# Local attention's values by two products and transfers, the common expert's first quarter in the tail of the chunked streams, and ScalarE's table loads placed by the planner

## The chip, the cores and the metric

The kernel runs on one core of a Trainium2 chip, in one launch. The metric is the device time of a launch in microseconds (us), the median of several runs. A profiled execution, from which all spans, waits and busy times are read, is a launch of its own with a time of its own. The engines are TensorE (PE, with its weight loads PEld), VectorE (DVE), ScalarE (ACT), GpSimd (POOL) and SyncE (SP), which here only issues transfers.

## The reference

The input is `x` of 8 sequences by 256 tokens by 128 channels (float32). Four layers follow each other, each an attention part and a feed-forward part, and each part ends in `x = layernorm(x + part(x))`. Some parts read the same 2048 tokens under another grouping.

```
L0 attn   gated linear recurrence (rglru), 4 x 512 tokens
L0 ffn    2 layers: local attention (8 heads of 64, window 64), then a gated MLP (gelu)
L1 attn   selective scan (mamba): exp(delta A), 16 states per channel
L1 ffn    32 experts, top 1, capacity 80
L2 attn   chunked streams: attention + ffn in chunks of 32 (la, lf), then across chunks (sa, pf)
L2 ffn    8 experts, top 2, capacity 320, and a common expert for every token
L3 attn   16 heads of 8, rotary and decay by head type, causal
L3 ffn    one matrix, quantized to -a, 0, +a
```

Two pieces matter here. Local attention, where a window of 64 queries sees its own 64 keys and the 64 before them:

```
q, k, v = split(shift_token(x) @ wqkv)
sim  = q_window . [k_window_before, k_window]      (masked: i < j or i > j + 64)
out  = softmax(sim) @ [v_window_before, v_window]
```

And the common expert of the L2 feed-forward, which reads all 2048 tokens and adds its result to that of the routed experts:

```
shared = silu(x @ sg) * (x @ su) @ sd              sg, su: 128 x 1024, sd: 1024 x 128
```

## The kernel before

**Stages.** The program is written as generators, one for each stage, which yield between steps: `rglru`, then local attention and the scan together (`local_mamba`, to about 800 us of the profile), `moe1`, `chunked` (to about 1270 us), `moe2`, and `typed`, which ends the kernel. `x` lies as channels by tokens (128 x 2048) in SBUF.

**Order.** Instructions are not issued in the order of the text. The class `_Order` collects all operations with their dependencies and makes a plan by list scheduling, with durations from a table (`LENGTHS`), a bias for each kind of operation and stage (`BIAS`), and a time that an engine stays with one kind of tile or one table (`STAY`). `impose` then chains each engine's operations in the planned order. So a change of one number in these tables may move instructions in every stage, and a queue, that of SP's transfers too, issues strictly in its planned order: an instruction that waits holds up all behind it. PSUM banks are handed out by stage and letter (`self.psum("Q", "vps")`); `chunked` has three of K, two of A, one of B and two of M, and `moe2` two of A, two of B, three of M and one of S.

**Local values.** `local_attention` runs for 2 layers by 8 sequences, 16 blocks of 256 tokens. Queries come in two tiles of 128. The first tile sees keys 0 to 127; in the second one the first 64 queries see keys 64 to 191 and the last 64 see keys 128 to 255. Keys on partitions are needed for the second product (`o`), so the values of keys 0 to 127, 64 to 191 and 128 to 255 are made by three products `vps`, each copied by ACT into a third of `v` (L1123 to 1128). The loads of `bc` that the scan of mamba multiplies with (L1269, 128 loads of 256 KB) stand in SP's queue in the same stage.

**The tail of `chunked` and `moe2`.** `chunked` passes 8 sequences through la, lf, sa and pf, several in flight. Each ends with `normed`, a transposition `zt`, the copy `x_chunked`, and the logits of the router (`lg`, then the positions by `cum`). After the last sequence come its scatters into `places` (POOL), two reads of `places` each (`got<-places`, some issued by ACT), the transposes `bt`, and the 8 experts (`pg<-bt`, `pu`, `py`). The common expert is made in four quarters of 512 tokens by `shared(i)`, a generator inside `moe2`: 8 chunks of 128 hidden channels, each of two products 128x512 (`pg`, `pu`), a Silu (ACT, L2052), a multiplication (DVE, L2057) and four products that add into one bank, `acc`. Quarter 0 covers the routing of the last sequence; quarters 1 to 3 come after the experts. During quarter 1 the gathers of the experts' results (`got<-ybuf,get`, POOL, L1658, 32 in this stage) are paced one a chunk by `fetch`; during quarters 2 and 3 the first sequence of `typed` is begun.

**Tables of ACT.** Exp and Ln share a table set; Silu, Gelu and Sigmoid each need another. A change of set puts an `ACT_TABLE_LOAD` into ACT's queue. Before Silu, Gelu or Sigmoid it is put in by itself; for Exp and Ln the text asks for the load by hand, with `exp_ln` (L900), right after the last activation of the other set, and `keep` holds it there.

Of the kernel before, what the change touches and what calls it, by code (L numbers as in the profile page):

```python
# [23 lines left out]
P = 128  # L24
B = 8
S = 256
# [55 lines left out]
def _tables():  # L82
# [65 lines left out]
    madd("band", np.concatenate([mask((i < k0) | (i > k0 + 64)), mask((k0 < w) | (k0 > w + 64))], 1))  # L148
# [163 lines left out]
class _Order:  # L312
# [14 lines left out]
    STAY = dict(PE=80, ACT=740)  # L327
    BIAS = {
        "ACT  1": 100, "ACT  5": 585, "ACT bt 3": 5, "ACT bt 5": -775, "ACT d 2": -425, "ACT da 2": -45, "ACT e 2": -5, "ACT e 4": 965, "ACT e 6": -20,
        "ACT got 3": 575, "ACT h 2": -200, "ACT ix 4": 15, "ACT k 2": 265, "ACT lavp 2": 210, "ACT lnrs 1": -10, "ACT lnrs 2": -160, "ACT lnsq 1": -135,  # L330
        "ACT lnsq 2": 15, "ACT ot 2": 10, "ACT ptsb 2": -595, "ACT ptsb 6": -515, "ACT q 2": 20, "ACT qsq 2": 10, "ACT r 2": -5, "ACT rg 1": 10,
        "ACT rg 2": -915, "ACT rn 2": 15, "ACT rs 4": 340, "ACT rs 6": -690, "ACT s 6": 200, "ACT sakq 2": -10, "ACT sg 3": -550, "ACT sh 5": -2525,
        "ACT spe 1": -220, "ACT spt 1": -50, "ACT st 6": 100, "ACT sz 2": 280, "ACT v 2": 885, "ACT vs 4": 320, "ACT xchunked 2": 15, "ACT xs 2": -610,
        "DVE biasfull 3": -335, "DVE biaspart 3": -20, "DVE bt 5": -5, "DVE c 1": 590, "DVE centre 0": 320, "DVE d 2": 10, "DVE decaypart 4": -600,
        "DVE e 4": 570, "DVE four 4": 100, "DVE fs 4": -70, "DVE gate 4": 340, "DVE get 2": 200, "DVE got 4": 530, "DVE identb 0": -50, "DVE k 6": 500,
        "DVE lg 2": 2240, "DVE lo 4": -265, "DVE mv 4": -660, "DVE mv 5": 100, "DVE mv 6": -485, "DVE nm 2": -3975, "DVE nm 6": 4960, "DVE nth 4": -45,
        "DVE oh 2": -725, "DVE oh 5": -10, "DVE ptsb 2": -3895, "DVE ptsb 6": 895, "DVE put 4": -395, "DVE put 5": 55, "DVE q 5": -825, "DVE q 6": -475,
        "DVE rc 2": -1225, "DVE rc 6": 10, "DVE route 2": -55, "DVE s 5": 10, "DVE sares 2": 70, "DVE sel 2": -1590, "DVE sg 3": -140, "DVE sm 4": 2720,
        "DVE spl 1": -215, "DVE ss 2": 370, "DVE st 4": 85, "DVE st 6": 1645, "DVE sum 4": 170, "DVE t 2": 440, "DVE u 2": 250, "DVE vs 4": 50,
        "DVE we 4": 1425, "DVE xc 2": 460, "DVE xla 4": -15, "DVE xlocal 2": -5, "DVE xmoe 5": -200, "DVE xmoe 6": -580, "DVE xpf 4": -370,  # L340
        "DVE xrglru 2": 120, "DVE xsa 4": 80, "DVE z 4": -1990, "PE a 2": -100, "PE acc 5": 155, "PE b 2": -35, "PE bt 3": 75, "PE bt 5": 50,
        "PE cum 2": -995, "PE cum 4": -25, "PE cum 5": -615, "PE fold 2": 2915, "PE g 2": -4155, "PE gate 2": 785, "PE kps 4": 135, "PE less 2": 295,
        "PE lg 2": 1680, "PE lg 4": 50, "PE ln 2": -10, "PE o 2": 10, "PE o 6": -10, "PE pg 5": 150, "PE ps 4": -15, "PE pt 4": -130, "PE pu 3": 220,
        "PE py 3": -200, "PE py 5": 170, "PE qk 2": 25, "PE qkt 2": -720, "PE raw 2": -8675, "PE rows 2": 400, "PE sc 2": -50, "PE sc 4": 65, "PE sc 6": 5,
        "PE v 5": 290, "PE vps 2": 4075, "PE vps 4": 25, "PE wo 2": 75, "PE wo 6": -85, "PE wout 2": -115, "PE xin 2": 1180, "PE xps 2": -2540, "PE y 2": 20,
        "PE z 2": -450, "PE zt 5": 560, "PE zt 6": 25, "POOL d 2": 130, "POOL e 6": -30, "POOL got 4": -200, "POOL h 2": 370, "POOL k 5": 400,
        "POOL k 6": 850, "POOL km 6": 1240, "POOL mean 0": 1510, "POOL places 5": -200, "POOL q 6": 20, "POOL rest 4": -65, "POOL rg 1": -800,
        "POOL rg 2": -200, "POOL rot 2": -400, "POOL s 6": -750, "POOL t 2": 550, "POOL zero 0": -655, "POOL zeros 1": 385, "SP bc 2": -970, "SP cst 3": 5,
        "SP got 3": 355, "SP got 5": 350, "SP rottable 0": 80, "SP rows 4": 210, "SP rowschunked 4": -105, "SP vec 0": -830, "SP w 0": 15, "SP w 3": 115,
        "SP wattn 2": 585, "SP wffn 2": 705, "SP wlocal 0": 1175, "SP wmoe 4": 520, "SP xs 2": -105, "SP ybuf 5": -200,  # L350
    }
    LENGTHS = {
        "ACT  LoadActFuncSet  ": (1178, 1283), "ACT d Ln 128x512 128x512": (535, 640), "ACT da Exp 128x255 128x255": (398, 503),
        "ACT e Abs 128x256 128x256": (460, 565), "ACT e Exp 128x128 128x128": (420, 525), "ACT e Exp 128x256 128x256": (461, 566),
        "ACT e Exp 128x512 128x512": (527, 632), "ACT four Exp 128x2 128x2": (100, 205), "ACT got DMACopy 128x512 128x512": (454, 3611),
        "ACT h TensorCopy 64x255 64x255": (295, 400), "ACT lnrs Exp 128x256 128x256": (315, 420), "ACT ot TensorCopy 128x512 128x512": (486, 591),
        "ACT qsq Square 128x512 128x512": (494, 599), "ACT r Relu 128x256 128x256": (460, 565), "ACT rg Exp 128x1020 128x1020": (1039, 1144),
        "ACT rg Exp 128x1024 128x1024": (998, 1103), "ACT rg Ln 128x1024 128x1024": (950, 1055), "ACT rn Exp 128x16 128x16": (110, 215),
        "ACT rn Ln 128x16 128x16": (112, 217), "ACT rs Exp 128x2 128x2": (96, 201), "ACT rs Ln 128x2 128x2": (98, 203),
        "ACT sh Silu 128x512 128x512": (492, 597), "ACT v TensorCopy 128x512 128x512": (485, 590), "ACT xc Identity 128x256 128x256": (460, 565),  # L360
        "ACT xc Silu 128x512 128x512": (526, 631), "ACT xchunked TensorCopy 128x256 128x256": (263, 368), "ACT xmoe Identity 128x256 128x256": (404, 509),
        "ACT xs TensorCopy 33x256 33x256": (257, 362), "ACT xsq Square 128x128 128x128": (297, 402), "DVE biaspart TensorCopy 96x256 96x256": (197, 282),
        "DVE decay TensorScalarPtr 128x512 128x512": (508, 593), "DVE decaypart TensorCopy 128x512 128x512": (331, 416),
        "DVE four TensorScalarPtr 128x4 128x4": (76, 160), "DVE ge TensorScalarPtr 128x256 128x256": (380, 465),
        "DVE ge TensorScalarPtr 85x256 85x256": (372, 457), "DVE got TensorScalarPtr 128x128 128x128": (258, 343),
        "DVE h TensorTensor 128x256 128x256": (312, 397), "DVE hs TensorScalarPtr 128x1024 128x1024": (2189, 2274),
        "DVE hs TensorTensor 128x1024 128x1024": (1116, 1201), "DVE mv BNStatsAggregate 128x2 128x6": (82, 167),
        "DVE nm TensorTensor 128x8 128x8": (66, 151), "DVE ptsb TensorCopy 128x512 128x512": (589, 674), "DVE rc Reciprocal 128x16 128x16": (160, 245),
        "DVE rc Reciprocal 128x4 128x4": (84, 169), "DVE rc Reciprocal 128x8 128x8": (106, 191), "DVE rg TensorScalarPtr 128x256 128x256": (577, 662),
        "DVE rg TensorTensor 128x1024 128x1024": (1109, 1194), "DVE rottable TensorScalarPtr 128x256 128x256": (261, 346),  # L370
        "DVE s TensorScalarPtr 128x128 128x128": (247, 332), "DVE s TensorTensor 128x256 128x256": (323, 408),
        "DVE sm TensorReduce 128x16 128x512": (593, 678), "DVE ss TensorReduce 128x8 128x512": (594, 679), "DVE st BNStats 128x6 128x128": (197, 282),
        "DVE sum TensorReduce 128x32 128x448": (810, 895), "DVE t TensorScalarPtr 128x256 128x256": (384, 469),
        "DVE t TensorTensor 128x512 128x512": (593, 678), "DVE vec TensorTensor 128x1 128x1": (59, 144), "DVE vec TensorTensor 85x1 85x1": (59, 144),
        "DVE vs TensorCopy 128x512 128x512": (594, 679), "DVE wlocal TensorScalarPtr 128x682 128x682": (481, 566),
        "DVE x TensorScalarPtr 128x256 128x256": (368, 453), "DVE xc TensorScalarPtr 128x254 128x254": (383, 468),
        "DVE xc TensorScalarPtr 128x255 128x255": (384, 469), "DVE xla TensorScalarPtr 128x256 128x256": (442, 527),
# [65 lines left out]
    def group(self, i):  # L443
# [5 lines left out]
        if e == "ACT":  # L449
            return 1 if op == "LoadActFuncSet" else self.SETS.get(str(x.func).split(".")[-1]) if op == "Activation" else None  # L450
        return None

    def change(self, i):
        x, e, op = self.ops[i]
        if e == "ACT":
            return 0.0 if op == "LoadActFuncSet" else self.TABLE
# [315 lines left out]
class _Kernel:  # L772
# [125 lines left out]
    def exp_ln(self, last=None):  # L898

        i = self.nc.scalar.preload_act_table_set("natural_log_exp_and_others")  # L900
        if last is not None:
            self.issue_after([i], last)
# [1508 lines left out]
```

## Time and profile before

| | |
|---|---|
| median of 3 runs | 1628.3 us (1627.46 to 1633.44) |
| profiled execution | 1644.68 us, span 1642.9 us |
| granted clock of PE, mean | 0.942 |
| busy PE / DVE / ACT / POOL | 1417.4 / 1102.3 / 968.6 / 587.5 us |
| table loads in the five largest groups of them | 30, 16, 7, 3 and 2 |
| moved by DMA | 77.97 MB, mean 47 GB/s |

A row of the groups reads: line, engine, operation, out<-in, shapes, count, then busy time in us and the mean in ns of one, then the idle time of the engine ahead of them and what ended most of it. "L870" is the helper that issues every matmul, so its rows are told apart by their tiles. A float32 product of 128x512 shows as two MATMUL rows. In a timeline a row has its start, its length, the engine and the operation, and in brackets the idle time before it and its releaser.

### The profile page before, as it was taken

The numbers are of one execution on the slowest core, as the hardware profiler recorded it, in microseconds if no ns is written. First come the engines' busy times: TensorE is split into PE (matmuls) and PEld (weight loads), VectorE is DVE, ScalarE is ACT, GpSimd is POOL, SyncE is SP. The second block draws the span as 40 slices with busy tenths as digits, with TensorE's granted clock in tenths as the row PEclk, the third lists the DMA queues.
The fourth block names the chain that finished last, engine by engine and source line by source line (L and its number), as shares of the span: only waits on it lengthen the run. The fifth ranks groups of instructions, "written<-read, shape, count | busy, mean of one in ns | idle before, by whom it ended". The sixth has DMA issues, their size and how long they took to land. (4 is left out here: it accounts for less than half of the span.)

```text
span 1642.9 us, 28581 instructions
## 1 busy us (share of the span) xinstructions
PE 1417.4 (86%) x10826; PEld 909.4 (55%) x10826; DVE 1102.3 (67%) x2182; ACT 968.6 (59%) x2656; POOL 587.5 (36%) x535
## 2 busy tenths in 40 slices
PE   2688998989898887777579999999998899899997
PEld 1354554545554544334366766777675576556664
DVE  5745568898989898698545557554546333279886
ACT  3777888787978869446125545455453222167775
POOL 1334544535462523101431222212212102467774
PEclk7789999989999999779789999999998899999998
DMA  5000012121212223155430000000000130000000
GB/s 199 1 1 1 1 40 65 40 60 45 65 40 65 53 52 91 52 179 189 151 119 1 8 12 11 10 5 8 32 18 24 46 121 26 26 9 8 5 8 11
DMA packets 45113, 77.97 MB, mean 47 GB/s; under 512 B 5580, under 2 KB 21988, under 8 KB 43824
## 3 DMA queue, kind: packets, MB, share of 16 engines
q1 hardware_dynamic: 39648, 70.02, 14.0%
q0 software_dynamic: 3216, 5.07, 1.1%
q8 instruction: 85, 1.39, 0.4%
q10 hardware_dynamic: 2112, 1.05, 0.2%
q14 instruction: 52, 0.43, 0.1%
HBM read 66.87 MB, written 10.76 MB: 47 GB/s over the span
## 5 line engine op out<-in xcount | busy, mean ns | idle before, releaser
L870 PE MATMUL y<-hs,ident 128*128 128x512 f32 x256 | 139.7, 659 | 35.9 <-DVE hs L1307 35.6
L1158 POOL TENSOR_TENSOR e<-e,rc 128x1024 f32<-128x1024 f32 x32 | 78.0, 2437 | 202.7 <-DVE rc L1157 194.3
L1306 DVE TENSOR_TENSOR_SCAN hs<-da,hs 128x1024 f32<-128x1024 f32 x64 | 149.1, 2331 | 0.2
L2259 ACT ACTIVATE e<-sc,nm 128x128 f32<-128x128 f32 (+1 forms) x256 | 105.2, 427 | 46.6 <-DVE nm L2254 40.3
L1153 ACT ACTIVATE e<-sc,nm,rn 128x128 f32<-128x128 f32 x256 | 114.3, 466 | 13.8 <-DVE nm L1148 13.5
L981 PE MATMUL pt<-ident,e 128*128 128x128 f32 x768 | 114.2, 278 | 9.4 <-POOL e L1158 4.9
L1302 ACT ACTIVATE da<-d,na 128x255 f32<-128x255 f32 x256 | 109.3, 504 | 17.5 <-DVE hs L1306 13.7
L1836 POOL TENSOR_TENSOR e<-e,rc 128x512 f32<-128x512 f32 x32 | 34.0, 1064 | 219.8 <-DVE rc L1835 154.2
L981 PEld LDWEIGHTS pt<-ident,e 128*128 128x128 f32 x768 | 88.5, 141 | 42.5 <-issue 16.1
L2262 POOL TENSOR_TENSOR e<-e,rc 128x1024 f32<-128x1024 f32 x48 | 90.8, 1896 | 39.1 <-DVE rc L2261 32.1
L1105 POOL TENSOR_TENSOR t<-t,t 128x512 f32<-128x512 f32 x64 | 83.9, 1316 | 58.0 <-DVE t L1092 51.6
L1811 ACT COPY kp<-kps 128x512 f32<-128x512 f32 x128 | 74.7, 583 | 49.0 <-PE kps L870 46.4
L1658 POOL DMA_INDIRECT got<-ybuf,get x48 | 45.7, 952 | 159.2 <-DMA ybuf<-ys 97.1
L870 PEld LDWEIGHTS y<-hs,ident 128*128 128x128 f32 x256 | 48.5, 205 | 82.5 <-DVE hs L1307 54.2
L1304 DVE TENSOR_TENSOR hs<-u,bc 128x1024 f32<-128x1024 f32 x64 | 84.3, 1328 | 2.9 <-POOL u L1291 2.9
L1307 DVE TENSOR_TENSOR hs<-hs,bc 128x1024 f32<-128x1024 f32 x64 | 80.6, 1260 | 0.0
L1847 ACT COPY vs<-vps 128x512 f32<-128x512 f32 x64 | 37.4, 585 | 67.1 <-PE vps L870 53.6
L983 DVE COPY ptsb<-pt 128x512 f32<-128x512 f32 x104 | 68.8, 675 | 11.6 <-PE pt L981 9.3
L870 PE MATMUL qk<-w_local,h 128*128 128x512 f32 x128 | 69.3, 631 | 7.5 <-DVE t L1092 7.1
L870 PE MATMUL vps<-sa_vp,x_lf 128*32 128x512 f32 x512 | 68.4, 594 | 0.0
L1847 DVE COPY vs<-vps 128x512 f32<-128x512 f32 x64 | 43.3, 682 | 37.2 <-PE vps L870 25.1
L2057 DVE TENSOR_TENSOR sh<-sh,pu 128x512 f32<-128x512 f32 x32 | 22.0, 688 | 67.1 <-PE pu L870 54.0
(380 smaller groups left out, 3782.4 us busy)
## 6 DMA issues: line engine op xcount, KB each, us to landing
bc<-xs SPq DMA_DIRECT2D x128, 256.0 KB
w_moe<-in_e_dram SPq DMA_DIRECT2D x16, 768.0 KB
w_attn<-in_w_dram SPq DMA_DIRECT2D x4, 1024.0 KB
w_local<-in_w_dram SPq DMA_DIRECT2D x2, 1557.0 KB
places<-zeros SPq DMA_DIRECT2D x2, 1280.0 KB
got<-places SPq DMA_DIRECT2D x6, 256.0 KB
ybuf<-ys SPq DMA_DIRECT2D x8, 160.0 KB
x_in<-in_x_dram SPq DMA_DIRECT2D x1, 1024.0 KB
```

The source lines that it names most:

```text
L870: return self.nc.tensor.matmul(out, lhsT, rhs, start=start, stop=stop)
L981: self.last = self.nc.tensor.transpose(pt[:, j * P : (j + 1) * P], src[:, j * P : (j + 1) * P], self.ident)
L1105: nc.gpsimd.tensor_add(t1, t1, t2)
L1153: nc.scalar.activation(e[:, j, g, :], scs[:, j, g, :], AF.Exp, bias=nm[:, j, g : g + 1], scale=rq[:, j, g : g + 1], accum_out=sm[:, j, g : ...
L1158: nc.gpsimd.tensor_tensor(e, e, rc.unsqueeze(3).to_broadcast([P, 2, 4, P]), ALU.mult)
L1302: nc.scalar.activation(da[:, n, c, 1:S], d[:, c, 1:S], AF.Exp, scale=na[:, i : i + 1])
L1304: nc.vector.tensor_tensor(hs, u.unsqueeze(1).to_broadcast(shp), bn, ALU.mult)
L1306: nc.vector.tensor_tensor_scan(line(hs), line(da), line(hs), 0.0, ALU.mult, ALU.add)
L1307: nc.vector.tensor_tensor(hs, hs, cn, ALU.mult)
L1847: i = copy(v[:, c, :, :].rearrange("p a b -> p (a b)"), ps)
L2259: nc.scalar.activation(e[:, i, :], sc[:, i, :], AF.Exp, bias=nm[:, i : i + 1], accum_out=sm[:, i : i + 1])
L2262: nc.gpsimd.tensor_tensor(e, e, rc.unsqueeze(2).to_broadcast([P, n, keys]), ALU.mult)
```

## The change

**Local values.** Only keys 0 to 127 and 128 to 255 are multiplied and copied (two products). The middle tile is put together by two transfers from SBUF to SBUF on SP's queue, each of 64 partitions by 512: keys 64 to 127 go to partitions 64 to 127, where they already lie, and keys 128 to 191 to partitions 0 to 63, where they lie. The middle tile so has its halves swapped; the `k` columns of the second query tile's first half are read with halves swapped, and its half of the mask `band` is rolled by 64.

**Common expert.** `shared` becomes a method. Quarter 0 is made as `early` inside `one_sequence` for the last sequence of `chunked`, in `chunked`'s banks K and M, in steps between that sequence's `ffn`, `normed` and `x_chunked`; its sum lies in a part added to the tile of the weights. In `moe2`, quarter 1 stands where quarter 0 stood, quarters 2 and 3 after the experts; the gathers are paced two a chunk in quarter 2 and one in quarter 3, and the first sequence of `typed` begins in quarter 3.

**Tables.** `exp_ln`, `keep` and the loads by hand go. The planner counts a load for each change of set, and `impose` puts one in where ACT's planned order turns to Exp or Ln.

**Planner.** `BIAS` and `LENGTHS` are replaced (some 200 numbers); `STAY` goes from PE 80 and ACT 740 to PE 170 and ACT 530 ns.

```diff
     w = i % 64
-    madd("band", np.concatenate([mask((i < k0) | (i > k0 + 64)), mask((k0 < w) | (k0 > w + 64))], 1))
+    late = mask((k0 < w) | (k0 > w + 64))
+    late[:64] = np.roll(late[:64], 64, 1)
+    madd("band", np.concatenate([mask((i < k0) | (i > k0 + 64)), late], 1))
...
-    STAY = dict(PE=80, ACT=740)
+    STAY = dict(PE=170, ACT=530)
...
     def impose(self):
         order, _ = self.plan()
+        ring, last = [], None
+        for i in order["ACT"]:
+            g = self.groups[i]
+            if g is not None:
+                if g == 1 != last:
+                    load = self.tc.nc.scalar.preload_act_table_set("natural_log_exp_and_others")
+                    self.ops.append((load.ins, "ACT", "LoadActFuncSet"))
+                    ring.append(len(self.ops) - 1)
+                last = g
+            ring.append(i)
+        order["ACT"] = ring
...
-            self.exp_ln(nc.scalar.activation(xc, xc, AF.Silu))
+            nc.scalar.activation(xc, xc, AF.Silu)
...
         v = pools.tile([P, 3, 512], F32, tag="v", name="v")
-        for a in range(3):
+        for t in range(2):
             ps = self.psum("Q", "vps")
-            self.mm(ps, h[:, 64 * a : 64 * a + P], w[:, l, 1024:1536])
-            nc.scalar.copy(v[:, a, :], ps)
+            self.mm(ps, h[:, t * P : (t + 1) * P], w[:, l, 1024:1536])
+            half = slice(64 - 64 * t, P - 64 * t)
+            nc.scalar.copy(v[:, 2 * t, :], ps)
+            nc.sync.dma_start(v[half, 1, :], v[half, 2 * t, :])
...
-                        self.mm(scs[q0 - t * P : q0 - t * P + n, j, g, :], q[r, g, q0 : q0 + n], k[r, g, k0 : k0 + P], False, g == 3)
+                        keys = k[r, g, k0 : k0 + P]
+                        if k0 == 64:
+                            keys = keys.rearrange("p (a b) -> p a b", a=2)[:, ::-1, :]
+                        self.mm(scs[q0 - t * P : q0 - t * P + n, j, g, :], q[r, g, q0 : q0 + n], keys, False, g == 3)
...
+                early = iter(())
                 if b == B - 1:
                     self.weights_shared()
+                    self.norm = None
+                    early = self.shared(0, y, self.s0, work, ("K", "M"), tag="e", bufs=4)
...
+                next(early, None)
                 z = yield from self.ffn(x3, w[:, 1, :], "pf", add, work, small)
+                next(early, None)
+                next(early, None)
                 zt = self.by_channel(z)
...
+                next(early, None)
                 yield 0.3, 0.6
...
                 z = self.normed(out[:, 0:2, :], work, small, "z")
+                next(early, None)
+                next(early, None)
                 yield 0.3, 2.5
...
                 nc.scalar.copy(y[:, cs], self.by_channel(z))
+                for _ in early:
+                    pass
                 yield 0.3, 0.8
...
+    def shared(self, i, x, s, work, banks=("A", "S"), tag="sh", bufs=None):
+        gu, down = self.wsh
+        acc = self.psum(banks[1], "acc")
+        nc.sync.dma_start(s, self.zrows[512 * i : 512 * (i + 1), :].rearrange("(t p) d -> p t d", p=P))
+        for c in range(8):
+            pg, pu = self.psum(banks[0], "pg"), self.psum(banks[0], "pu")
+            self.mm(pg, gu[:, 0, c * P : (c + 1) * P], x[:, cs])
+            self.mm(pu, gu[:, 1, c * P : (c + 1) * P], x[:, cs])
+            h = work.tile([P, 512], F32, tag=tag, name="sh", bufs=bufs)
+            self.silu = nc.scalar.activation(h, pg, AF.Silu)
...
+            self.paced = nc.vector.tensor_mul(h, h, pu)
+            for t in range(4):
+                ts = slice(t * P, (t + 1) * P)
+                self.mm(acc[:, ts], h[:, ts], down[:, c * P : (c + 1) * P], c == 0 and t == 0, c == 7 and t == 3)
+            yield
...
-            common = shared(0)
+            common = shared(1)
...
-            for _ in shared(1):
-                next(fetch)
             self.x = y
             first = chain(results(0, self.ty), self.typed_before(0))
             for i in (2, 3):
                 for _ in shared(i):
-                    next(first, None)
+                    next(fetch, None)
+                    if i == 3:
+                        next(first, None)
                     next(fetch, None)
```

## The prediction

> **What bounds the kernel now.** I read the page's busy shares first, then the busy time in windows cut by stage, then the groups of the edited lines, then the timelines of TensorE (PE) and ScalarE (ACT) in the tail of `chunked`.
>
> ```profile
> PE 1417.4 (86%) x10826; PEld 909.4 (55%) x10826; DVE 1102.3 (67%) x2182; ACT 968.6 (59%) x2656; POOL 587.5 (36%) x535
> 100.00:240.00 140.00, 124.69 (x888) 76.75 (x887) 78.59 (x141) 112.10 (x316) 62.42 (x72) 0.99 0.01 4
> 300.00:600.00 300.00, 263.27 (x1531) 156.10 (x1532) 270.35 (x337) 247.75 (x649) 140.90 (x121) 0.98 0.21 57
> 1249.90:1273.50 23.60, 16.73 (x87) 11.49 (x87) 18.91 (x115) 8.63 (x34) 8.48 (x10) 0.82 0.15 41
> 1273.50:1300.80 27.30, 22.02 (x97) 13.88 (x96) 8.16 (x24) 6.85 (x11) 7.93 (x9) 0.84 0.27 70
> 1360.00:1442.00 82.00, 73.10 (x328) 47.19 (x326) 25.79 (x54) 18.59 (x29) 34.09 (x35) 0.94 0.10 28
> ```
>
> The first line is the page's, the others are windows (stretch, its length, then busy time of PE, PEld, DVE, ACT, POOL, the granted clock, DMA). PE leads the whole, but not every stage. From 100 to 240 us, local attention before the scan, PE is busy 89% of the time, ACT 80%, VectorE (DVE) 56%: a product taken away there shortens the stage. From 300 to 600 us the scan runs beside it: DVE 90%, PE 88%, ACT 83%. A product saved there mostly becomes idle time of PE. The tail of `chunked` (1249.9 to 1273.5, one sequence left) has PE at 71% and ACT at 37%: here lies room for other work.
>
> ```profile
> L870 PE MATMUL vps<-w_local,h 128*128 128x512 f32 x96 | 52.4, 642 | 6.7 <-ACT v L1128 5.8 <-DVE t L1092 0.9
> L1128 ACT COPY v<-vps 128x512 f32<-128x512 f32 x48 | 28.0, 594 | 12.9 <-PE vps L870 12.7
> L900 ACT ACT_TABLE_LOAD x30 | 38.5, 1283 | 0.5
> L2052 ACT ACTIVATE sh<-pg 128x512 f32<-128x512 f32 x32 | 19.1, 597 | 76.4 <-PE pg L870 56.6 <-remote 11.5 <-issue 6.3
> ```
>
> Groups (count, busy us and mean ns, idle before and its releaser). A 128x512 product is two matmul rows: 96 rows for 48 products. The copies of `v` cost 594 ns, a table load 1283 ns, a Silu 597 ns. Silu waits for PE, hence PE bounds the common expert.
>
> ```profile
> 1275.13 0.20 ACT L1606 ACTIVATE four<-four 128x2 f32<-128x2 f32 x1 [3.56 <-DVE four L1605]
> 1275.35 1.28 ACT L2052 ACT_TABLE_LOAD   x1
> 1276.64 0.60 ACT L2052 ACTIVATE sh<-pg 128x512 f32<-128x512 f32 x1
> 1282.44 1.02 ACTq L1643 DMA_DIRECT2D got<-places  x2
> 1283.50 0.60 ACT L2052 ACTIVATE sh<-pg 128x512 f32<-128x512 f32 x1 [6.26 <-issue]
> 1277.29 2.08 PE L870 MATMUL pg<-x_chunked,w_shared 128*128 128x512 f32 x2 [3.58 <-ACT sh L2052]
> ```
>
> ACT's and PE's timelines. The first Silu of the common expert waits for the last exp of the routing and a load; the second waits 6.26 us, since ACT's queue holds the two reads of `places` until the scatters have landed. PE stands 3.58 us here and its clock was granted at 0.50 from 1265 to 1282. So 50.9 us (1249.9 to 1300.8) pass from the tail's last `zt` to the experts, with 38.75 us of PE work at a mean clock of 0.83.
>
> ```profile
> 1411.11 1.02 PE L870 MATMUL pg<-x_chunked,w_shared 128*128 128x512 f32 x2
> 1411.97 1.02 PE L870 MATMUL pu<-x_chunked,w_shared 128*128 128x512 f32 x2
> 1412.17 0.60 ACT L2052 ACTIVATE sh<-pg 128x512 f32<-128x512 f32 x1 [2.01 <-PE pg L870]
> 1414.78 0.60 ACT L2052 ACTIVATE sh<-pg 128x512 f32<-128x512 f32 x1 [2.01 <-PE pg L870]
> ```
>
> In steady state a product steps by 0.86 us (1411.97 - 1411.11) and a chunk by 2.61 us (1414.78 - 1412.17). A quarter has 8 chunks: 20.9 us, all PE.
>
> **Local values.** 16 blocks (2 layers, 8 sequences) lose one product and one copy each: 16 x 0.86 = 13.8 us of PE, 16 x 0.594 = 9.5 us of ACT. The built order also has five loads fewer before `chunked` (65 to 60): 6.4 us of ACT. Eight blocks have their products before 245 us, where PE decides: 8 x 0.86 x 0.89 (PE's share) = 6.1 us gained. For the other eight DVE is as busy as PE; between nothing and 6.9 us I take a quarter, 1.7. Sum -7.8. The best end is all of the product time and the loads, -13.8 - 6.4 = -20.2: one row speaks for the loads, PE's 4.29 us of idle at 61.1 us, waiting for a copy of `v` while ACT does six loads in 14 us.
>
> Added are 32 transfers of 128 KB on SP's queue. Issue: the 256 KB loads of `bc` took a median of 0.42 us each there, so 13.6 us on a queue that does little else. Landing: the trace has no such transfer; the nearest is the reading of `places` (256 KB), issued at 1282.4 with its transposes at 1288.6, at most 6.2 us. The cover: in before's 16 blocks 8.7 to 40 us lie between the last copy of `v` and the first `o` product of the second query tile, which is what needs the moved rows. So the landing costs nothing; with the cover gone it is 6.2 us a block at most. The swapped halves and the rolled mask change no size of a product. The wait that is added: each transfer stands in SP's order behind its ACT copy, and behind it stand loads of `bc` that DVE's scan needs. Those loads are double-buffered (they wait for DVE, 175 us in all), so I price this at zero; the bad end is a rival below.
>
> **First quarter in the tail.** Let X be the time from 1249.9 to the last routing product `cum`, 23.6 us now. In the built order all 8 pairs of products and the 32 `acc` products of quarter 0 stand before that `cum`, and ACT goes back and forth 7 times between Silu and exp/ln: 14 loads in place of none. ACT's work: 8.63 + 14 x 1.283 + 8 x 0.597 = 31.4 us. PE's: 16.73, less the one chunk already there (four rows from 1269.9, about 3.6), plus 20.9: 34 us at the worst clock seen, some 31 at full clock. So X is at least 31.4; with every load and Silu put onto the chain it is 23.6 + 18.0 + 4.8 = 46.4. Between them neither engine excludes either end; I take the middle, 38.9. From `cum` to the experts 27.3 us stay: 8 scatters in a row on POOL (1.27 us each), the reads, the transposes; quarter 1 now covers them as quarter 0 did (22.0 us of PE work in them now, 20.9 of it a quarter's). Then behind the experts two quarters are left of three: -20.9. Sum 38.9 + 27.3 - 50.9 - 20.9 = -5.6; ends -13.1 (X = 31.4) and +1.9 (X = 46.4). The products wait in banks of `chunked` (two of three K, one of two M), so the sequence's own `ffn` and transposes are served by what is left: part of why I do not take 31.4. The weights' loads were issued at 1184 and 1193 us, 57 us ahead: no cost.
>
> A load's price is the row's 1283 ns: the Silu starts 0.01 us after it, and the load 0.02 us after the exp. The Trainium skill speaks against this interleaving ("ScalarE: Activation LUTs", sections "What ACT_TABLE_LOAD costs" and "Table sets: the hidden batching unit"): it puts a switch at about 2.7 us with its drain, and has calls batched by set. By that the 14 loads would be 37 us, the serial X 65, and this part a loss of some 21 us at that end. The trace shows no drain, so the row goes into the sum.
>
> **Gathers.** 32 gathers step by 1.25 us (0.95 and 0.30 of issue): 40 us from 1381.6, beside 62.7 us of quarters. Now they run beside 41.8 us, two a chunk, and the first sequence's `q`, `k`, `km` stand among them on POOL. They come in order of sequence, so only some start late: 0 to 3 us, I take 1. Loads behind the experts lie beside an ACT that is busy 18.6 of 82 us: nothing.
>
> **New order.** Biases and stays are retuned, so every stage is reordered; built tile-shape switches of PE rise by some 20. No row prices an order; the longest single wait of PE for the scan (`y` after `hs`) is 5.2 us, and one such wait more or less is what I allow, +-5, centre 0.
>
> Sum: -7.8 - 5.6 + 1 = -12.4. The profiled execution took 1644.7 us (span 1642.9 and 1.8 around it), 16.4 above the median; one stall in it (ACT 11.5 us, "remote", near 1391 to 1403) I neither credit nor count. It would go to 1632.3; as a difference from the median: 1628.3 - 12.4 = **1616**.
>
> **Rivals.** (1) Everything gains: -20.2 - 13.1 + 1 = -32, so 1596. For it: ACT and PE are both lightened at once in the first stage, and PE's half clock in the tail goes when it is fed. Against: DVE at 90% from 300 to 600 us.
> (2) One half gives nothing: the local products hide behind the scan and the new order (1623), or X comes out at 44.5, where the tail neither gains nor loses (1621). For it: the serial X of 46.4.
> (3) SP's queue, slower:
>
> ```profile
> SPq L1269 <- DMA xs<-xs: 9.5, 8, 2.2
> L1269 SPq DMA_DIRECT2D bc<-xs x128: 319/423/1637, 236.9 to 779.0; - x128
> ```
>
> (waits of SP's queue: us in all, times, longest; and the `bc` loads, ns min/median/max, first and last start.) The eight blocks beside the scan put 16 transfers among these 128 loads. If each holds the next `bc` for the longest landing wait seen, 2.2 us, DVE loses 35 us: -12.4 + 1.7 + 35 = +24, 1653. It turns the change into a loss from 0.7 us per transfer, and by over 0.5% from 1.2. Against: the loads are issued ahead.
> (4) The change does not save table loads, as it says it plans them: the built count rises from 69 to 76. That is in X.
>
> **Numbers.** 0.5%, about what a measurement of this kernel can tell, is 8.1 us: faster is under 1620.2, slower over 1636.4. My forecast with its +-8 (1608 to 1624) has 0.50, of it 0.36 faster; rival (1) 0.20, faster; rival (2) 0.14, of it 0.11 same; rival (3) and a tail worse than its bound 0.16, slower. So 0.59, 0.25, 0.16. Range 1596 (rival 1) to 1640 (rival 3 at 1.4 us a transfer).
>
> **What would show it.** Right: 64 rows of `vps<-w_local,h` and 32 copies of `v`; PE's share from 100 to 240 no lower and the scan's first `hs` earlier; 24 Silus behind the last `cum`, with X near 39 and PE's clock above 0.82 in it; `sc` of `typed` about 12 us earlier. Wrong: DVE idle before `hs` released by `bc`; PE idle before `o` released by a transfer of `v`; X over 46; loads with idle time ahead of them; or stages that the edit does not touch (`moe1`, `chunked` before 1184, `typed`) moving by more than 5 us, which would put the retuned order above my three parts.

## The result and the profile after

The changed kernel takes 1641.3 us (median of 4 runs, 1637.3 to 1642.5) against 1629.1 for the kernel before (4 runs, 1627.5 to 1633.4): ratio 1.0064, interval 1.0044 to 1.0084. In a later series it took 1636.5 us (12 runs) against 1631.2: ratio 1.0036, 1.0018 to 1.0054. So it is slower by 0.4 to 0.6%, where 0.8% faster was forecast.

Its profiled execution has a span of 1635.5 us, 7 less than the one shown for the kernel before. That one was not typical: profiled again, the kernel before has 1628.9 (first experiment). All that follows is compared with this second profile.

Page (busy) and windows of the changed kernel; the columns are as in the prediction.

```profile
PE 1417.8 (87%) x10794; PEld 903.1 (55%) x10794; DVE 1091.4 (67%) x2182; ACT 972.7 (59%) x2647; POOL 584.2 (36%) x535
```

```profile
100.00:240.00 140.00, 120.55 (x824) 74.95 (x824) 73.89 (x135) 106.34 (x303) 59.73 (x70) 0.94 0.05 11
300.00:600.00 300.00, 260.31 (x1526) 153.23 (x1525) 265.34 (x337) 243.74 (x632) 137.31 (x117) 0.98 0.24 63
1244.80:1280.40 35.60, 33.66 (x182) 23.22 (x182) 24.53 (x123) 27.90 (x54) 10.57 (x12) 1.00 0.09 21
1280.40:1306.00 25.60, 22.41 (x89) 12.23 (x86) 7.38 (x23) 6.85 (x11) 5.91 (x7) 0.93 0.28 73
1418.00:1635.00 217.00, 201.67 (x1698) 116.78 (x1698) 162.64 (x394) 135.05 (x606) 134.99 (x87) 0.98 0.02 7
```

The same stretches of the tail and of `typed` in the second profile of the kernel before:

```profile
1244.40:1268.30 23.90, 17.04 (x89) 11.70 (x89) 18.93 (x115) 8.63 (x34) 8.67 (x10) 0.81 0.14 40
...
1428.00:1628.00 200.00, 185.20 (x1698) 111.91 (x1698) 161.30 (x394) 133.71 (x606) 132.91 (x86) 0.97 0.03 8
```

In the tail PE does 33.7 us of work in 35.6, at full clock; before it had 17.0 in 23.9 at 0.81. In `typed` the number of PE's rows is the same (1698), but they are busy for 201.7 us instead of 185.2. Groups of the edited lines, as in the prediction:

```profile
L765 ACT ACT_TABLE_LOAD x38 | 48.8, 1283 | 0.6
L879 PE MATMUL vps<-w_local,h 128*128 128x512 f32 x64 | 32.9, 608 | 0.0
L2041 ACT ACTIVATE sh<-pg 128x512 f32<-128x512 f32 x32 | 19.1, 597 | 48.8 <-PE acc L879 36.8 <-PE pg L879 11.9
L1123 ACT COPY v<-vps 128x512 f32<-128x512 f32 x32 | 18.4, 591 | 3.3 <-PE vps L879 3.3
```

The products and copies are gone as planned (64 rows of 96, 32 copies of 48). Stage by stage, from the times at which the first or last instruction of a tile stands in each trace:

| stage, up to | before | after | difference | forecast |
|---|---|---|---|---|
| local attention and scan, last `lg` | 801.8 | 798.9 | -2.9 | -7.8 |
| `moe1`, last `py` | 37.6 | 47.0 | +9.4 | 0 |
| `chunked`, last `out<-sa_res` | 405.0 | 398.9 | -6.1 | 0 |
| tail, first `py` of the experts | 55.6 | 66.0 | +10.4 | +15.3 |
| experts and quarters, first `sc` | 128.0 | 107.2 | -20.8 | -19.9 |
| `typed`, last computing instruction | 196.3 | 212.9 | +16.6 | 0 |

The sum is +6.6. The rows that hold the three parts of the change that I had priced bring 13.3 us, and `chunked` 6.1 more; two stages that I had priced at nothing take 26.0 back. A second trace of the changed kernel (below) has the first row at 803.9 (+2.1) and `moe1` at 42.0 (+4.4), the other rows within 0.6 us of these, and the same sum within 0.2: a single trace's first and second row are uncertain by some 5 us.

The first row starts at zero and holds `rglru` too. Counted from the first local product `qk` (46.6 us before, 43.1 after) to the scan's last `y` (794.2, 791.7), local attention and scan take 747.6 us before and 748.6 after: the 2.9 us lie ahead of the first local product, where the change to the values has no part. The nine traces of kernels that share this stage's instructions and biases with the changed one give 748.6 to 750.9 us, the two of the kernel before 747.6 and 747.8.

**Where `moe1` lost.** ACT's timeline of the kernel before (second profile), then the changed kernel's ACT and PE:

```profile
805.22 0.26 ACT L1532 ACTIVATE lg<-lg 128x64 f32<-128x64 f32 x1 [3.39 <-DVE lg L1531]
805.49 1.28 ACT L1535 ACT_TABLE_LOAD   x1
...
816.55 0.44 ACT L1707 ACTIVATE sg<-pg 128x320 f32<-128x320 f32 x1 [2.15 <-PE pg L870]
```

```profile
802.28 0.26 ACT L1529 ACTIVATE lg<-lg 128x64 f32<-128x64 f32 x1 [2.70 <-DVE lg L1528]
...
816.19 1.28 ACT L1699 ACT_TABLE_LOAD   x1 [3.83 <-PE pg L879]
817.48 0.44 ACT L1699 ACTIVATE sg<-pg 128x320 f32<-128x320 f32 x1
...
817.97 1.57 PE L879 MATMUL pg<-bt,w_moe 128*128 128x80 f32 x6 [0.80 <-ACT sg L1699]
```

Before, the load for Silu followed the routing's Exp at once and was done 10 us ahead. After, it is put in by itself in front of the first Silu and only starts when that Silu's input is there: 3.83 us of waiting, then the load. PE gets a gap of 0.80 us, and in these two traces its clock stays low for longer (windows, after, then before; the last but two column is the clock):

```profile
820.50:825.50 5.00, 5.00 (x26) 5.00 (x26) 1.08 (x2) 0.88 (x2) 0.00 (x0) 0.50 0.01 3
825.50:830.50 5.00, 5.00 (x26) 5.00 (x26) 0.49 (x1) 0.59 (x1) 0.00 (x0) 0.50 0.00 0
```

```profile
817.50:822.50 5.00, 5.00 (x41) 5.00 (x40) 2.28 (x5) 1.39 (x3) 0.39 (x1) 0.84 0.01 3
822.50:827.50 5.00, 5.00 (x48) 5.00 (x47) 2.36 (x4) 0.88 (x2) 0.00 (x0) 1.00 0.74 234
```

**Where `typed` lost.** PE's timeline, changed kernel:

```profile
1499.69 1.12 PE L879 MATMUL sc<-km,q 64*128 64x512 f32 x2
1500.75 0.44 PE L956 MATMUL zt<-ident,s 128*128 128x128 f32 x2
1501.11 0.69 PE L879 MATMUL sc<-km,q 64*128 64x512 f32 x1
1501.12 0.39 PE L879 MATMUL sc<-decay,onesb 64*128 64x512 bf16 x1
1501.65 0.59 PE L879 MATMUL sc<-km,q 64*128 64x512 f32 x1
```

A pair of score products uses 64 rows each, on the two halves of the array. Next to each other the four rows of a pair take 1.06 us together. Here a `zt` stands between the two, and each takes as long alone as both together (1.06 us from 1499.69 to 1500.75). 15 of the 48 pairs are parted so, by `zt` or `wo`, whose biases in this stage the retuning had made more urgent (25 to -1090 and -85 to -845); before, none is.

### The profile page after: what moved, and what is told of

It is laid out like the page before. It is cut to its first block, busy times and chain, and to the rows that moved or that the text cites. A ratio compares the mean times of both kernels' runs of the same rounds, so it can differ in the third digit from the quotient of the medians.

```text
span 1635.5 us, 28604 instructions
## 1 busy us (share of the span) xinstructions
PE 1417.8 (87%) x10794; PEld 903.1 (55%) x10794; DVE 1091.4 (67%) x2182; ACT 972.7 (59%) x2647; POOL 584.2 (36%) x535
## 4 chain that ended last, share of the span: by engine, by line
PE 56%; DVE 19%; ACT 13%; issue 6%; POOL 5%; DMA 2%; ACTq 0%; SPq 0%; DVEq 0%; POOLq 0%
PE sc L879 9%; PE vps L879 7%; PE kps L879 6%; PE out L879 4%; PE pt L976 4%; DVE hs L1304 4%; ACT e L1152 4%; PE pu L879 3%; PE pg L879 3%; DVE hs L1302 2%; PE o L879 2%; DVE hs L1305 2%; ACT da L1300 2%; PE py L879 2%; PE y L879 2%
## 5 line engine op out<-in xcount | busy, mean ns | idle before, releaser
L879 PE MATMUL y<-hs,ident 128*128 128x512 f32 x256 | 146.2, 683 | 35.7 <-DVE hs L1305 35.5
L1305 DVE TENSOR_TENSOR hs<-hs,bc 128x1024 f32<-128x1024 f32 x64 | 77.2, 1211 | 0.0
L879 PE MATMUL sc<-km,q 64*128 64x512 f32 x192 | 70.7, 640 | 0.9 <-DVE s L2052 0.9
L978 ACT COPY ptsb<-pt 128x512 f32<-128x512 f32 x88 | 51.5, 585 | 28.3 <-PE pt L976 23.9
L879 PE MATMUL sc<-msk,identb 128*128 128x512 bf16 (+2 forms) x224 | 49.5, 361 | 20.7 <-ACT e L1152 20.4
## 6 DMA issues: line engine op xcount, KB each, us to landing
v<-v SPq DMA_DIRECT2D x32, 128.0 KB, 2.2
```

Source lines behind the costliest of these rows:

```text
L879: return self.nc.tensor.matmul(out, lhsT, rhs, start=start, stop=stop)
L978: copy(sb.rearrange("p a b -> p (a b)"), pt)
L1305: nc.vector.tensor_tensor(hs, hs, cn, ALU.mult)
```

## The experiments

**The kernel before, again.** No edit. 

> The kernel before, profiled once more. Theory: its first profiled execution (1644.7 us) held a disturbance that its other executions (median about 1629) do not have, the 11.5 us stall of ACT and PE near 1391 to 1403 above all. Then this span is 1626 to 1632, the stall is gone, and all other stages end where they did, within 2 us. Rival: the profile itself costs 16 us; then the span is near 1643 again and the stall stands in its place.

1630.7 us, span 1628.9; the 11.5 us stall is gone, and `chunked` is 6.6 us shorter than in the first profile. The first profiled execution was disturbed; its stage times must not be used for differences.

**The load of `moe1` early.** In `impose`, for `moe1` alone (`at` is the place behind the last Exp, Ln or Silu):

```diff
+                if g == 2 != last and self.stage[i] == 3:
+                    load = self.tc.nc.scalar.preload_act_table_set("silu_and_others")
+                    self.ops.append((load.ins, "ACT", "LoadActFuncSet"))
+                    ring.insert(at, len(self.ops) - 1)
```

> The changed kernel with one instruction moved: moe1's one load of the Silu table goes from just ahead of the first Silu back to just behind the routing's Exp, where the kernel before had it; nothing else moves. Theory: the load stood on moe1's path behind the wait for the first product, gave PE a gap of 0.8 us and kept its clock at half until 833 us instead of 820; without it moe1 ends 7 to 8 us earlier and the whole is 5 to 8 us faster than the changed kernel (about 1634). Rival: moe1 lost its 9 us to the new order of its products (the down products come late); then only the load itself is saved, 0 to 1.5 us.

1635.3 us (9 runs), 6.0 below the changed kernel's first median, 1.2 below its second. In the trace the gap is gone and `moe1` takes 41.4 us instead of 47.0. The clock still rises later than before (window of this kernel):

```profile
822.50:827.50 5.00, 5.00 (x33) 5.00 (x32) 1.57 (x3) 0.87 (x2) 0.00 (x0) 0.67 0.02 3
```

How late it rises differs between traces too. From `moe1`'s first `bt` to its last `py` it takes, with the load late, 35.3 us (changed kernel), 35.2 (next experiment) and 30.3 (the changed kernel again, below); the clock is back at 1.00 at 23, 23 and 13 us after that `bt`. With the load early it takes 29.7 us in three traces and 25.7 in one (the doubled product), with the clock back at 13 and at 3 us. So where the clock rises equally soon, at 13 us, the load's place is worth 0.6 us (30.3 against 29.7). The other 5 us go with a clock that rises 10 us later. That the late load causes this is not shown: one trace has the late load, its gap of 0.80 us and the earlier rise. Between medians of one series, with the pairs of the next experiment kept in both, the load's place is worth 1.8 us (1623.6 against 1621.9), which is within their intervals.

**The pairs of `typed` kept.** In `impose`, what stands between the two halves of a pair is put behind the second:

```diff
+        order["PE"] = self.paired(order["PE"])
...
+        for i in ring:
+            if half(i):
+                out.append(i)
+                second = not second
+            else:
+                (late if second else out).append(i)
+            if not second:
+                out, late = out + late, []
```

> The changed kernel with 15 products of typed moved by a few places on PE: the two score products of a pair (64 rows each, on the two halves of the array) stand next to each other again, in all 48 pairs; a foreign product that stood between them comes after them. Nothing else moves. Theory: two such products run side by side when adjacent (0.01 us apart in the trace) and one after the other when parted (0.5 us and 0.4 us more), and typed is bound by PE; so 15 x 0.9 = 13 us faster than the changed kernel (about 1628). Rival: typed is held by DVE, ACT and POOL as much as by PE, and the time goes into waits: 0 to 4 us faster.

1623.6 us (8 runs; ratio to before 0.9963, 0.9949 to 0.9977). `typed` takes 201.3 us instead of 212.9. PE's timeline and the group, this kernel, and the group of the changed kernel:

```profile
1496.43 1.13 PE L893 MATMUL sc<-km,q 64*128 64x512 f32 x4
1497.49 0.44 PE L970 MATMUL zt<-ident,s 128*128 128x128 f32 x2
```

```profile
L893 PE MATMUL sc<-km,q 64*128 64x512 f32 x192 | 54.0, 640 | 0.9 <-DVE s L2066 0.9
```

```profile
L879 PE MATMUL sc<-km,q 64*128 64x512 f32 x192 | 70.7, 640 | 0.9 <-DVE s L2052 0.9
```

Count and mean are the same, 640 ns; only the busy time tells that rows overlap (54.0) or do not (70.7). Moving 15 products by a few places is worth 11.6 us in the trace, and 13 to 18 between medians; within one series, with the load early in both, 13.5 (1635.3 against 1621.9). Why trace and medians differ is not known.

**Both.** 

> Both moves together. Theory: they lie in different stages and add up: 18 to 21 us faster than the changed kernel, 1619 to 1623, below the kernel before by 6 to 10. Rival: 1 to 5 us faster than the changed kernel.

1621.9 us (5 runs; 0.9952, 0.9932 to 0.9971). With two placements mended the change is faster than the kernel before.

**The changed kernel, again.** 

> The changed kernel as it is, for a time on the same chip as the next three. Expected 1637 to 1642 by every theory; by the stages: moe1 and typed each longer than before by 9 and by 16 us, all other stages shorter.

1636.5 us (12 runs), span 1636.0. The first stage ends 5.0 us later than in its first trace, `moe1` takes 42.0 us instead of 47.0, and all other stages agree within 1.5 us: `typed` has its 212.4.

**A local product twice.** On both moves; the twins are not planned, but spliced in behind their firsts:

```diff
             one = self.mm(ps, h[:, t * P : (t + 1) * P], w[:, l, 1024:1536])
+            if t == 0:
+                self.twin(self.mm(ps, h[:, t * P : (t + 1) * P], w[:, l, 1024:1536]), one)
...
+            one = nc.scalar.copy(v[:, 2 * t, :], ps)
+            if t == 0:
+                self.twin(nc.scalar.copy(v[:, 2 * t, :], ps), one)
```

> The kernel with both moves (load early, pairs kept), in which the first of the two local products of each of 16 blocks, and its copy, are made twice, each twin right behind its first; the order of everything else is held fixed. This adds 16 products of 0.86 us to PE and 16 copies of 0.59 us to ACT, what the change had taken away. My prediction's theory (PE decides in the first eight blocks, a quarter of the rest): 6 to 10 us slower than with both moves. The theory after the traces (the saved products became idle time of PE before the softmax of the same block, the stage won 2.9 us only): 1 to 5 us slower.

1632.5 us (12 runs). Both moves did not run in this series, so the traces are compared: the scan's last `y` comes at 805.8 against 791.9: 13.9 us, as much as 16 x 0.86; the last instruction at 1622.9 against 1614.9, 8.0. Of this, 0.8 us lie ahead of the first `qk`, about 4 between it and the scan's first `hs` (six blocks, 5.2 us of products) and about 9 beside the scan (ten blocks, 8.6). In sum the added products and copies were on the stage's path, though not all of it reached the end: this was the trace whose `moe1` took 25.7 us, 4.0 of the difference. The theory that I had after the traces (1 to 5 us) falls.

**The small product.** The kernel before in its own order, the middle tile's product and copy of a block (the second of three in the text) cut to 8 columns, with their planned cost kept. The middle tile's values are so left out, and no transfer stands in their place; the outputs read the last tile's instead:

```diff
-            self.mm(ps, h[:, 64 * a : 64 * a + P], w[:, l, 1024:1536])
-            nc.scalar.copy(v[:, a, :], ps)
+            n = 8 if a == 1 else 512
+            self.mm(ps[:, 0:n], h[:, 64 * a : 64 * a + P], w[:, l, 1024 : 1024 + n])
+            nc.scalar.copy(v[:, a, 0:n], ps[:, 0:n])
...
-                        self.mm(o[64 * j : 64 * j + 64, g, qs], v[:, a, hd * 64 : (hd + 1) * 64], pt[:, g, qs])
+                        self.mm(o[64 * j : 64 * j + 64, g, qs], v[:, 2 if a else 0, hd * 64 : (hd + 1) * 64], pt[:, g, qs])
```

> The kernel before, in its own order held fixed, in which the third local product and copy of each of the 16 blocks are cut from 512 columns to 8 (the middle tile's values are not computed; its outputs read the last tile's instead), without any transfer. This takes away what the change took away, and moves nothing. My prediction's term: 6 to 9 us faster than before. Theory after the doubled product (under a fixed order every product is on the path): 10 to 14 us faster. Rival, the saved product becomes a wait for the softmax: 0 to 4 us faster.

1623.2 us against 1628.3 (12 and 27 runs; 0.9974, 0.9954 to 0.9994). The last `y` comes 7.5 us earlier, at 786.7, or 6.5 counted from the first `qk`; the medians differ by 5.2. But the first `hs` of the scan comes at 248.8 against 249.1: the six blocks whose products stand ahead of it give 0.3 us at most, the ten beside it the rest. The theory taken from the doubled product (10 to 14) falls in its turn; adding a product in one order and taking one away in the other are not worth the same, and whether the order or the direction makes the difference is not shown.

**Quarter 0 late.** On both moves, with moe2's biases of before; the pacing of the gathers and the start of `typed`'s first sequence go back with the quarter:

```diff
-                    early = self.shared(0, y, self.s0, work, ("K", "M"), tag="e", bufs=4)
...
-            common = shared(1)
+            common = shared(0)
```

> The kernel with both moves, in which quarter 0 of the common expert is made where the kernel before made it (in moe2, with moe2's biases of before), and the other quarters and the gathers too. Theory by the stages of the traces (the tail 10 us longer with the quarter in it, what follows the experts 20.6 shorter): 9 to 12 us slower than with both moves. My prediction's term: 5.6 us slower. Rival, the tail is bound by ACT's table loads: no slower, or faster.

1644.7 us. It tells little: the order it got waits for the gathers right behind the experts.

```profile
1392.16 0.91 PE L1137 MATMUL zt<-ident,s 128*128 128x128 f32 x2 [12.17 <-DVE s L1131]
```

Its `typed`, with the changed kernel's biases, takes 200.9 us: so the 5 us that `typed` keeps too many with the pairs mended do not come from the quarter's place. It was run again with the other biases for moe2, on the best kernel below:

> The preceding kernel with quarter 0 of the common expert made in moe2 as before, now with the changed kernel's biases for moe2, in whose order the first sequence's transposition comes eight chunks after the experts and not at once (the wait of 12 us of the last such run should be gone). Theory: 9 to 12 us slower than the preceding kernel. My prediction's term: 5.6 us slower. Rival, the tail is bound by table loads: no slower.

1631.2 us against 1618.4 (12 and 6 runs): 12.8 us slower. In the traces the last instruction comes at 1625.0 against 1612.3, 12.7. That is what quarter 0 in the tail is worth, the pacing of the gathers included, in the orders that the planner finds for the two places.

**Old biases for `moe1` and `typed`.** 

> The kernel with both moves, and with the planner's biases of the kernel before for moe1 and for typed alone, so that these two stages are ordered nearly as before. Theory: what the two moves left of their losses, 3.8 us in moe1 and 5 us in typed, is the retuned order too; 5 to 9 us faster than with both moves, near 1614. Rival: the 5 us in typed come from the change (the first sequence's inputs begin a quarter later, so less is ready when its scores start); then 3 to 4 us faster.

1632.9 us. `moe1` takes 26.7 us from its first `bt` to its last `py` instead of 29.7, the time of the kernel before; but `typed` takes 214.1 instead of 201.3, though no pair is parted. So the old biases are no safe way back: `moe1` gains by them in the changed program, and `typed` loses.

**The best version.** Both moves and the old biases for `moe1` alone. 

> The kernel with both moves (load early, pairs kept), and with the biases of before for moe1 alone. Theory: the last run's loss against both moves lay in typed alone (214 against 201 us), its moe1 took the 26.7 us of before against 29.7; so this is both moves less 3 us, 7 to 12 us faster than before. Rival: the gain of both moves over before was one chip's, and it is within 4 us of before.

1618.4 us (6 runs; 0.9938, 0.9917 to 0.9960): 10 us faster than the kernel before, and faster than the changed one by 18 to 23.

**Every load early.** As in the first move, for all sets and stages. 

> The preceding but one kernel (both moves and moe1's biases), in which every load of a table, of Silu, Gelu and Sigmoid too, is put right behind the last activation of the other set instead of ahead of the first of its own. Theory: only a load whose activation waits for its input was on the path (moe1's, now moved; a wait of 1.5 us in front of a Silu of mamba and 0.4 in the tail); 0 to 3 us faster. Rival: loads stand on the path in many places; 5 us or more faster.

1621.1 us (10 runs), no better than the best version: the places of the other loads had nothing more to give.

**Transfers twice, and the old biases for the local stage.** Both on the best version.

```diff
+            self.twin(nc.sync.dma_start(self.spare[64 * n : 64 * n + 64, :], v[half, 2 * t, :]), one)
```

> The kernel with both moves and moe1's biases, in which each of the 32 transfers of local values is followed in SP's queue by a second one of the same 128 KB (to a spare tensor in memory); the order of everything else is held fixed. If the transfers cost what the changed kernel's local stage lost against the 7.5 us that the products are worth (it won 2.9), doubling them costs 2 to 5 us more at the end of the scan. Theory now: they are hidden, 0 to 1 us. The prediction's slower rival (0.7 to 2.2 us for each transfer beside the scan): 10 us or more.

> The same kernel with the biases of before for local attention and the scan too. If the new order of that stage is what lost 4.6 of the 7.5 us, its end (the last y of the scan) comes 3 to 6 us earlier than in the kernel with both moves and moe1's biases, counted from the first stage's end. If the loss belongs to the change itself (transfers, halves), it comes no earlier; biases tuned for three products may also fit two badly, and then it comes later.

Transfers twice: 1617.9 us (6 runs) against 1618.4; the last `y` at 791.3 against 792.6. So their issue and their transport cost nothing. A second transfer finds its copy already made, so this run does not double SP's wait for the copies; for that wait the traces are read below. Old biases: 1650.6 us; the last `y` comes 35 us later. It does not tell whether the new order of the stage lost what the products are worth.

## Why the prediction was wrong

**The step that failed is "New order".** I took every stage's reordering as +-5 us with centre 0, for want of a row that prices an order. Two stages lost 26.0 us by it in the first trace, 20.5 in the second, and two places could be read in the built orders that I had: the 15 parted pairs (11.6 us, third experiment) and the Silu load of `moe1`, which the diff no longer puts in by hand (second experiment: 0.6 us with the clock's rise at the same time, 1.8 between medians, 5.6 in traces where the clock also rose earlier). For the first a row existed: `sc<-km,q` shows 192 rows of mean 640 ns and 54.0 us busy, so rows run side by side, and an order that parts them must lose. For the second I had counted loads (69 to 76) and not asked, for each load that is no longer put in by hand, what its Silu waits for. The old biases give `moe1` another 3.0 us (29.7 to 26.7), so that is order as well. Why the clock rose late in two of the three traces with the late load stays open. The 5 us left in `typed`, and the 6.1 won in `chunked`, where the edit removes no work, are put down to the order without a run that isolates them.

**Tail: right, and better than forecast.** X came out at 35.6 us (38.9 taken, as the middle of the ends 31.4 and 46.4), near PE's own 33.7, with the clock at 1.00 instead of 0.81 now that PE was fed. ACT had 12 loads and 27.9 us of work there, not 14 and 31.4. The experts came 10.4 us later (15.3) and what follows was 20.8 shorter (20.9 for the quarter, less 1 for the gathers): -10.4 where -4.6 was forecast, and 12.8 by the experiment. ACT went back and forth at 1.28 us a load without drain:

```profile
1275.83 1.28 ACT L2041 ACT_TABLE_LOAD   x1
1277.41 0.60 ACT L2041 ACTIVATE sh<-pg 128x512 f32<-128x512 f32 x1 [0.30 <-PE pg L879]
1278.03 1.28 ACT L765 ACT_TABLE_LOAD   x1
1282.35 0.20 ACT L1598 ACTIVATE four<-four 128x2 f32<-128x2 f32 x1 [3.03 <-DVE four L1597]
```

The load at 1278.03 starts 0.02 us after the Silu and is done 3 us before its own exp has its input. The Trainium skill's price with drain ("ScalarE: Activation LUTs", "What ACT_TABLE_LOAD costs"), about 2.7 us, made X 65 at its end by the prediction's estimate; the measured 35.6 decides. Its advice to batch by set did not bind in the tail, where the 12 loads fitted beside PE's work.

**Local values: a second term that failed.** I took 7.8 us off the first stage. Counted from the first local product, the changed kernel needs 1.0 us more for it than the kernel before (748.6, 747.6). In the order of before, held fixed, the products are worth 6.5 to 7.5 us of the stage; that this is near the 7.8 is luck, since it lies in the other place: 0.3 at most in the blocks where PE was 89% busy (6.1 forecast), and about 7 beside the scan, where DVE was 90% busy (1.7 forecast). The count of blocks was wrong too: six blocks, not eight, have their products before 245 us, and ten come with the scan. Ahead of the scan the changed kernel's PE has 4.0 us less work (166.3 instead of 170.3 from the first `qk` to the first `hs`), but waits 16.2 us instead of 4.5 for the softmax's exp ahead of `sc`. PE's share from 100 to 240 us fell from 89% to 86%, where no fall was to be the sign of being right. The longest such wait for the exp, in the second profile of the kernel before, then in the changed kernel:

```profile
81.49 1.01 PE L870 MATMUL sc<-msk,identb 128*128 128x512 bf16 x2 [2.15 <-ACT e L1153]
```

```profile
76.64 1.01 PE L879 MATMUL sc<-msk,identb 128*128 128x512 bf16 x2 [11.52 <-ACT e L1152]
```

So a busy share of 89% did not mean that a product counts for 0.89: PE's saved work became its wait. How much of that wait belongs to the new order, and how much to the shorter products alone, no run separates.

**Rivals.** SP's queue, the slower one, is refuted. Doubling the transfers cost nothing, although 20 of them, not 16, stand beside the scan (ten blocks). A transfer lands 2.2 us after its issue, and no wait of PE in the stage is ended by a landing of `v`. SP sits 116 us waiting for copies of `v`, in 16 waits, and still DVE waits 2.1 us in all ahead of the scan's first operation, and not for `bc`. The changed kernel's page (the group of that operation, and the DMA issues) and the waits of SP's queue:

```profile
L1302 DVE TENSOR_TENSOR hs<-u,bc 128x1024 f32<-128x1024 f32 x64 | 81.4, 1286 | 2.1 <-POOL u L1289 2.1
...
v<-v SPq DMA_DIRECT2D x32, 128.0 KB, 2.2
```

```profile
SPq L1124 <- ACT v L1123: 116.1, 16, 49.6
```

None of my rivals held a loss in `moe1` or `typed`, stages that the edit's text does not touch; the last line of what would show me wrong, such a stage moving by more than 5 us, is what came.

**The profile that I differenced against** was itself 14 us too long (1642.9, then 1628.9). I carried over a difference and not a level, so this did not enter the sum; but a forecast checked on the two first profiles alone would have looked like a gain of 7 us.

## What to carry to other kernels

When an edit goes with a retuned schedule, compare the two built orders stage by stage for what depends on adjacency: half-array products side by side, and a table load that stands in front of a waiting activation. A table load is free where the engine waits after it and on the path where it waits ahead of it, so put it right behind the last use of the old set wherever the next use waits; in `moe1` this alone was worth 0.6 us with the clock alike. Before a stage's loss is blamed on a change, hold the order fixed and take away or double that one thing; a replanned run mixes both, and here a replan alone moved a stage by up to 35 us. Take a second trace of a kernel before a few microseconds of one stage are explained: here the first stage and `moe1` each differed by 5 us between two traces of the same program.

## What was not expected of the hardware

Two products of 64 rows on the two halves of the array, issued one after the other, take the time of one (0.01 us between their starts); one foreign product between them undoes it, 11.6 us for 15 pairs, 0.8 each. And PE's clock in `moe1` stayed at 0.50 for 23 us after the first `bt` in two traces with the load late, and for 13 us in the third, with PE never idle for more than 0.8 us; with the load early it was up after 13 us in three traces and after 3 in a fourth, with the old order after 6. The Trainium skill ("TensorE: Matmul & The Clock Gate", "What's actually happening") gives about 3.4 us of sustained work for the rise. Here the measured times decide; what holds the clock down is not settled by these runs.
